# A gated attention and expert block on one core: transposes moved from the DMA engines to TensorE, and the experts' down products regrouped

## The chip, the cores and the metric

The kernel runs on one core of a Trainium2 chip. The metric is the device time of one execution in microseconds; three timed runs of the kernel before gave 570.42, 572.45 and 572.47, the median is 572.45. The profile is of one further execution. Engines are named as in the profile: PE is TensorE, PEld its weight loads, DVE is VectorE, ACT is ScalarE, POOL is GpSimd, SP is SyncE, which here only issues DMAs.

## The reference, cut to what matters

Inputs are tokens `x` of 4 batches x 512 x 512 (H = 512), a wide weight per batch (`fside`, 512 x 512), a narrow weight per batch (`ctx`, 512 x 256), a router weight for 16 experts, three weights for each expert (I = 352), and a shared pair of layers (704 wide).

```python
def _smooth_quant_linear(x, w):          # per batch, int8 steps
    s = sqrt(max(amax_x, EPS) / max(amax_w, EPS)); xs = x / s; ws = w * s
    x_scale, w_scale = row maxima / 127
    x_q, w_q = round(xs / x_scale), round(ws / w_scale)
    return x_q @ w_q.T * x_scale * w_scale.T
...
x = x + tanh(g_xattn) * linear2(silu(gate) * up)        # gate, up = halves of linear1(layernorm(x))
t = layernorm(x)
top 2 of softmax(t @ gate_w.T); tokens sorted to 16 experts x 256 slots
expert_out = (silu(buf @ w_gate) * (buf @ w_up)) @ w_down
x = x + tanh(g_ffn) * (weighted sum of a token's two expert rows + shared layers(t))
```

## The kernel before, in words

**Stages.** The work falls into five stretches of the profile's time.

1. The opening, up to about 62 us, is batch 0's quantized layers, written out by hand as a list of steps with a rough time each (`opening.at`), and ends with `beside` (line 1316), which puts batch 1's first steps among the first chunk of batch 0's shared layers.
2. From 62 to 282 us a planner (`Plan`, before the kernel function) sets the order. Each step has an engine, a cost in us, the steps it needs, the buffers that it takes and gives, and a rank; the planner plays the engines forward and takes, among the steps that are ready, the one with the lowest rank. What it yields is only the order in which each engine's instructions stand; the engines then follow it strictly, each waiting for what its next instruction needs. Here run batches 1 to 3 of the quantized layers (`plan_first`, `plan_second`), the routing (`plan_scores`), and, with the highest rank numbers, the shared layers of batches 0 to 2 (`plan_shared`), which fill TensorE.
3. From 282 to 511 us the 16 experts follow each other in a loop (`gate_up`, `down_routed`, `turn_features`).
4. From 511 to the end come the shared layers of batch 3 and the gathering of the experts' rows into the result.

**Quantized layers.** `steps_x` (line 509) and `steps_w` (556) write int16 steps. A product needs them with the summed dimension in partitions, so they are turned. For batches 0 and 1, TensorE turns them as bf16 bit patterns into a PSUM bank, four or two 128x128 blocks for each of four tiles (`turn_tile`, line 356), and ScalarE or VectorE copies the bank to SBUF as numbers (`take_x`, `take_w`, `take_a`). For batches 2 and 3 (`BY_DMA`, line 363), SP issues DMA transposes of two tiles each (`send_pair`, 369), which land on the X-bar path, and VectorE casts the landed int16 to bf16 in place (`steps_to_float`, 380). `block` picks the matching layout for the product.

**Normalized tokens.** After the second layer, `normal` (746) writes a tile `y`. `keep_normal` (759) splits each f32 of `y` into two planes of 16 bits with a ScalarE copy, and `store_normal` (764) writes the planes to `xn_dram`. `plan_keep` (1429) plans both, for most tiles with a late rank. `turn_normal` (770) turns `y` on TensorE for the router and the shared layers.

**Experts.** For expert e, `gather(e, h)` (1102), issued on GpSimd's queue, fetches 128 rows of planes by index into `xg`; `send_tokens` (1129) issues a DMA transpose on SP's queue into `xp`; `join_tokens` (1133), a strided ScalarE copy, puts the planes together to `A`, the turned f32 tokens. Tokens of e + 1 are prepared while e is computed. `combine_tokens` (1136) and `combine_weights` (1086) make the sums and differences, on VectorE, with which gate and up need seven products in place of eight (a scheme of Winograd's kind); in `gate_up` (1183) they are written to four banks b1 to b4, and ScalarE and VectorE copies and adds gather them. b1 is accumulated on while copies are taken of it: each later product onto b1 stands behind a ScalarE copy. Then `down_tile` (1234) makes two tiles of 128 tokens x 512 from three chunks of the 352 features (128, 128 and 96 rows), `take_down` (1163) copies them out of PSUM and ScalarE's queue issues their store, and `turn_features` (1168) turns the gated features of e with six TensorE turns, which `join_features` (1177) copies to SBUF with VectorE. In the loop, expert e's gate and up stand first, then down of e - 1, then the turns of e:

```python
        for e in range(E - 1):
            gate_up(e)
            if e > 0:
                down_routed(e - 1)
            turn_features(e)
...
        gate_up(E - 1)
        down_tile(E - 2, 0)
        turn_features(E - 1)
        down_tile(E - 2, 1)
```

Weight loads from DRAM are issued on SP's queue two experts ahead (`load_gate`, `load_up`, `load_down`, from line 1071).

Of the kernel before, what the change touches and what calls it, by code (L numbers as in the profile page):

```python
# [12 lines left out]
I16 = mybir.dt.int16  # L13
# [107 lines left out]
def flamingo_gated_kernel(  # L121
# [32 lines left out]

    xn_dram = dram.tile([B * S, 2 * H], I16, tag="xn_dram", name="xn_dram")
# [207 lines left out]
    BY_DMA = (2, 3)  # L363

    def by_tile(dst):

        return dst.rearrange("p k s -> p (k s)").rearrange("p (t k q) -> p t k q", t=TT, q=P)

    def send_pair(dst, q, u):

        to = by_tile(dst.bitcast(I16))[:, 2 * u : 2 * u + 2].rearrange("p t k q -> p (t k) q")
        nc.sync.dma_start_transpose(out=to, in_=q[:, 2 * u : 2 * u + 2, :].rearrange("p t n -> p (t n)"))

    def block(b, dst, k, t=None):

        if b not in BY_DMA:
            return dst[:, k, :] if t is None else dst[:, k, bass.ts(t, P)]
        return by_tile(dst)[:, :, k, :] if t is None else by_tile(dst)[:, t, k, :]

    def steps_to_float(dst):  # L380

        vec.tensor_copy(dst, dst.bitcast(I16))

    def planes(on, dst, src):

        n = src.shape[1]
        copy_on(on, dst[:, :, :n], src.bitcast(I16).rearrange("p (n l) -> p l n", l=2))

    def turn_planes(dst, src):

        nc.sync.dma_start_transpose(out=dst, in_=src.rearrange("p l n -> p (l n)"))

    def join_planes(on, dst, src):

        copy_on(on, dst.bitcast(I16).rearrange("p k (s l) -> p l k s", l=2), src.rearrange("p (l k) s -> p l k s", l=2))

# [43 lines left out]
    def first(b):  # L440
# [93 lines left out]
        def send_x(u):  # L534
            send_pair(w.xqT, v.xq, u)

        def send_w(u):
            send_pair(w.wqT, v.wq, u)

        def sent_x():  # L540
            steps_to_float(w.xqT)

        def sent_w():
            steps_to_float(w.wqT)

# [24 lines left out]
        def product(t):  # L570
            if t == 0:
                w.a3 = qb.tile([P, TT, A], F32, tag="a3", name="a3")
                w.ama = qb.tile([P, A], F32, tag="ama", name="ama")
            accs[t] = chain_ps[1]([P, H], F32, "acc")
            for k in range(HC):
                pe.matmul(  # L576
                    accs[t], lhsT=block(b, w.xqT, k, t), rhs=block(b, w.wqT, k), start=(k == 0), stop=(k == HC - 1)
                )
# [37 lines left out]
    def second(b):  # L616
# [66 lines left out]
        def send_a(u):  # L683
            send_pair(v.xqT, v.xq, u)

        def send_w(u):
            send_pair(v.wqT, v.wq, u)

        def sent_a():
            steps_to_float(v.xqT)  # L690

        def sent_w():
            steps_to_float(v.wqT)

# [26 lines left out]
        def multiplied(t):  # L721
            if t == 0:
                v.mv = stat.tile([P, TT, 2], F32, tag="mv2", name="mv2")
            accs[t] = chain_ps[1]([P, H], F32, "acc2")
            for k in range(nk):
                pe.matmul(  # L726
                    accs[t], lhsT=block(b, v.xqT, k, t), rhs=block(b, v.wqT, k), start=(k == 0), stop=(k == nk - 1)
                )
# [28 lines left out]
        yps = {}  # L757

        def keep_normal(t, on=act):
            yp = qb.tile([P, 2, H], I16, tag="q", name="yp", bufs=2)  # L760
            planes(on, yp, ys[t])
            yps[t] = yp.rearrange("p l n -> p (l n)")

        def store_normal(t):
            j = b * TT + t
            nc.sync.dma_start(out=xn_dram[j * P : (j + 1) * P, :], in_=yps[t])
# [335 lines left out]
    def gather(e, h):  # L1102
        c = e * (CAP // P) + h
        R[e].xg[h] = xg = ep.tile([P, 2, H], I16, tag="xg", name="xg", bufs=3)
        pool.indirect_dma_start(  # L1105
            out=xg.rearrange("p l n -> p (l n)"),
# [8 lines left out]
    def open_routed():  # L1115
        home.A = shp.tile([P, 2, CAP // P, HC, P], F32, tag="xT", name="xgT", bufs=2)
        home.S4 = qb.tile([P, 4, HALF, P], F32, tag="a3", name="S4")
        home.xp = [ep.tile([P, 2 * HC, P], I16, tag="xp", name="xp", bufs=2) for _ in range(CAP // P)]
# [10 lines left out]
    def send_tokens(e, h):  # L1129
        R[e].A = home.A[:, e % 2]  # L1130
        turn_planes(home.xp[h], R[e].xg[h])

    def join_tokens(e, h, on=act):
        join_planes(on, R[e].A[:, h], home.xp[h])
# [42 lines left out]
    def join_features(e, h):  # L1177
        r = R[e]
        if h == 0:
            r.hT = qb.tile([P, len(CHUNKS_I), CAP], F32, tag="wc", name="ehT", bufs=2)  # L1180
        vec.tensor_copy(r.hT[:, :, bass.ts(h, P)], r.tps[h][:, : len(CHUNKS_I), :])

    def gate_up(e):
# [7 lines left out]
        if e > 1:  # L1191
            take_down(e - 2, 1)
        for h in range(CAP // P):
            if two_more:
                gather(e + 2, h)
            if more:
                send_tokens(e + 1, h)
        product(b1, r.A11, r.Bg, True)
        act.copy(p1, b1)
        product(b2, r.A12, r.Dg, True)  # L1200
        if two_more:
# [8 lines left out]
        if e > 0:  # L1210
            for h in range(CAP // P):
                join_features(e - 1, h)
# [4 lines left out]
        product(b4, r.S4, r.Du, True)  # L1217
        if two_more:
# [3 lines left out]
        if more:  # L1222
            for h in range(CAP // P):
                join_tokens(e + 1, h)
        product(b1, r.A22, r.T4, False)
        act.activation(g2, b1, AF.Silu)
        for step in weights[2:]:
            step()
        vec.tensor_tensor(home.h[1][:, :I], g2, u3, ALU.mult)
        if more:  # L1230
            for step in combine_tokens(e + 1):
                step()

# [6 lines left out]

    def down_routed(e):
        for h in range(CAP // P):
            down_tile(e, h)
        take_down(e, 0)
        if e + 2 < E:
            load_down(e + 2)
# [63 lines left out]
    for t in range(TT):  # L1310
        opening.at(61.0 + 0.5 * t, lambda t=t: s0.normal(t, vec), lambda t=t: s0.turn_y(t))
# [4 lines left out]
    def beside():  # L1316
# [3 lines left out]
        order += up[:2] + [f1.row_rs, f1.row_s, *each(f1.multiply), *each(f1.divide)] + up[2:] + [times]  # L1320
# [4 lines left out]
    opening.at(65.0, beside, lambda: s0.keep_normal(TT - 1), lambda: s0.store_normal(TT - 1))  # L1325
# [10 lines left out]
    SENT = 1.8  # L1336

    def plan_sent(send, sent, us, steps, q, rank, needs=()):

        landed = []  # L1340
        for u in range(TT // 2):
            issue = plan.add("SP", 1.3, lambda u=u: send(u), *steps[2 * u : 2 * u + 2], *needs, rank=rank)
            landed.append(plan.add("XBAR", 0.8, nothing, issue, rank=rank, gives=[q]))
        done = plan.add("DVE", us, sent, *landed, rank=rank)
        done.late = SENT
        return [done]
# [14 lines left out]
    def plan_first(b, f, wide, narrow, began):  # L1361

        add, r = plan.add, b * 1000.0
        by_dma = b in BY_DMA
# [30 lines left out]
        if by_dma:  # L1395
            turns, took = [], plan_sent(f.send_x, f.sent_x, 0.7, steps, q, r + 10, [first_last[b - 1]])
        else:
            o = add("PE", 0.0, f.open_x, steps[0], rank=r + 10, takes="tp", count=2)
            turns = [add("PE", 0.27, lambda t=t: f.turn_x_tile(t), steps[t], o, rank=r + 10, gives=[q]) for t in range(TT)]
            took = [add("ACT", 1.02, lambda: f.take_x(0, act), *turns, rank=r + 11, gives=[o]), add("DVE", 0.7, lambda: f.take_x(2, vec), *turns, rank=r + 11, gives=[o])]  # L1400
# [5 lines left out]
        if by_dma:  # L1406
            took += plan_sent(f.send_w, f.sent_w, 0.7, steps, q, r + 13, [first_last[b - 1]])
        else:
            o = add("PE", 0.0, f.open_w, steps[0], *turns, rank=r + 13, takes="tp", count=2)
            turns = [add("PE", 0.27, lambda t=t: f.turn_w_tile(t), steps[t], o, rank=r + 13, gives=[q]) for t in range(TT)]  # L1410
            took += [add("ACT", 1.02, lambda: f.take_w(0, act), *turns, rank=r + 14, gives=[o]), add("DVE", 0.7, lambda: f.take_w(2, vec), *turns, rank=r + 14, gives=[o])]
# [17 lines left out]
    def plan_keep(s, t, y, rank):  # L1429

        kept = plan.add("ACT", 1.1, lambda t=t: s.keep_normal(t), y, rank=rank, takes="q2", gives=[y])
        sent = plan.add("SP", 0.45, lambda t=t: s.store_normal(t), kept, rank=rank)
        STORED.append(plan.add("XBAR", 0.0, nothing, sent, rank=rank, gives=[kept]))
        STORED[-1].late = 2.3

    def plan_second(b, s, first):
# [14 lines left out]
        by_dma = b in BY_DMA  # L1451
        steps = [add("ACT", 0.5, step, n, rank=r + 1) for step in each(s.steps_a)]
        A_free[b + 1] = steps[-1]
        if by_dma:
            took = plan_sent(s.send_a, s.sent_a, 0.43, steps, q, r + 1)
        else:
            o = add("PE", 0.0, s.open_a, steps[0], rank=r + 1, takes="tp")
            turns = [add("PE", 0.22, lambda t=t: s.turn_a_tile(t), steps[t], o, rank=r + 1, gives=[q]) for t in range(TT)]
            took = [add("ACT", 1.02, lambda: s.take_a(act), *turns, rank=r + 1, gives=[o])]
# [4 lines left out]
        if by_dma:  # L1464
            took += plan_sent(s.send_w, s.sent_w, 0.43, steps, q, r + 2)
        else:
            o = add("PE", 0.0, s.open_w, steps[0], rank=r + 2, takes="tp")
            turns = [add("PE", 0.22, lambda t=t: s.turn_w_tile(t), steps[t], o, rank=r + 2, gives=[q]) for t in range(HC)]
# [398 lines left out]
```

## Time and profile before

| What | Value |
|---|---|
| median of three runs | 572.45 us (570.42 to 572.47) |
| the profiled execution | 570.75 us, of which the span (first to last instruction) is 568.7 |
| granted TensorE clock, mean | 0.987 |
| DMA transposes | 32 of routed tokens, 16 of steps |
| ScalarE copies `xgT<-xp` | 31, 1.34 us each |
| ScalarE copies `yp<-y` | 16, 1.05 us each |
| VectorE casts after a DMA transpose of steps | 8, 0.41 to 1.33 us each |
| POOL waiting for `xp<-xg` before a gather | 161.0 us in 16 waits |

The profile's parts give busy time by engine (1), the span in 40 slices (2), DMA queues (3), the chain of work that ended last, followed back from the last instruction (4), and instruction groups with the idle time before them (5). Queries of the trace give the same for a stretch, an instruction list in order of time, and the chain piece by piece. Matmuls are pipelined: the mean length of one in a group is longer than the distance between two, so prices are taken from pieces of the chain.

### The profile page before, as it was taken

Reading aid. Unit: us, or ns where it says so; the run is one execution under the profiler, and the core shown is the slowest. Engines: PE = TensorE matmul, PEld = TensorE weight load, DVE = VectorE, ACT = ScalarE, POOL = GpSimd, SP = SyncE. Lnnn points to the kernel's source line nnn. Section 1 sums busy time; section 2 is a strip of 40 time slices with the busy share of each in tenths; the row PEclk is TensorE's granted clock in tenths of the full one; section 3 lists DMA queues with packets and bytes.
Section 4 is the critical chain, followed back from the end, with each engine's and each line's share of the span. In section 5 each row is a group of like instructions: output and inputs, shape, how many; then the busy total and the mean of one; then the engine's idle time right before and its main releaser. Section 6 shows DMA issues by size and latency. Waiting matters only on the chain.

```text
span 568.7 us, 6298 instructions
## 1 busy us (share of the span) xinstructions
PE 536.9 (94%) x1946; PEld 297.6 (52%) x1946; DVE 423.4 (74%) x976; ACT 234.1 (41%) x399; POOL 140.2 (25%) x155
## 2 busy tenths in 40 slices
PE   3786799999999999999989999999999999999997
PEld 2653444544445454454455555555555555557852
DVE  6999788999998998986278666666666666535887
ACT  4464567537626173060136444444444444422310
POOL 1315032253151511200320111111111110006771
PEclk8699999999999999999999999999999999999999
DMA  8981012012304184010676999999999989315778
GB/s 275 373 260 37 1 74 75 0 39 75 73 1 76 37 281 131 5 74 1 142 208 226 265 266 259 269 257 262 283 265 265 262 255 250 101 55 166 197 234 311
DMA packets 93969, 95.09 MB, mean 167 GB/s; under 512 B 51552, under 2 KB 70240, under 8 KB 93936
## 3 DMA queue, kind: packets, MB, share of 16 engines
q1 hardware_dynamic: 84064, 69.39, 44.6%
q0 software_dynamic: 5120, 16.78, 9.4%
q10 hardware_dynamic: 4752, 8.52, 4.0%
q8 instruction: 16, 0.26, 0.2%
q14 instruction: 17, 0.14, 0.1%
HBM read 66.36 MB, written 16.78 MB: 146 GB/s over the span
## 4 chain that ended last, share of the span: by engine, by line
PE 84%; DVE 12%; issue 1%; ACT 1%; DMA 1%; POOL 0%; SPq 0%; DVEq 0%
PE b L1154 23%; PE eo L987 15%; PE sh L1037 11%; PE pg L972 9%; PE pu L972 9%; PE b L1732 4%; PE pr L1011 2%; PE tp_h L1174 2%; PE acc L576 2%; PE sh L1043 1%; PE rowb L307 1%; DVE scx L331 1%; DVE xn L494 1%; PE tp_am L299 1%; PE acc L726 1%
## 5 line engine op out<-in xcount | busy, mean ns | idle before, releaser
L987 PE MATMUL eo<-wd,ehT 128*128 128x512 f32 (+1 forms) x192 | 85.1, 592 | 0.0
L1105 POOL DMA_INDIRECT xg<-xn_dram,slot_token x32 | 34.6, 1082 | 195.8 <-DMA xp<-xg 161.0
L1037 PE MATMUL sh<-wsd,hT 128*128 128x512 f32 x160 | 73.9, 597 | 0.0
L987 PEld LDWEIGHTS eo<-wd,ehT 128*128 128x128 f32 (+1 forms) x192 | 36.4, 190 | 41.6 <-issue 36.5
L972 PE MATMUL pg<-xT,wsg 128*128 128x512 f32 x120 | 57.4, 599 | 0.7 <-ACT xT L354 0.7
L972 PE MATMUL pu<-xT,wsu 128*128 128x512 f32 x120 | 56.5, 596 | 0.0
L1203 DVE TENSOR_TENSOR p<-p,b 128x352 f32<-128x352 f32 x16 | 8.3, 520 | 59.4 <-PE b L1154 59.4
L354 ACT COPY xgT<-xp 128x1024 int16<-128x1024 int16 x31 | 39.5, 1339 | 24.5 <-DMA xp<-xg 24.4
L1784 POOL DMA_INDIRECT yk<-eo_dram,slot x32 | 33.2, 1038 | 52.2 <-PE b L1732 42.8
L1037 PEld LDWEIGHTS sh<-wsd,hT 128*128 128x128 f32 x160 | 28.9, 190 | 30.9 <-issue 28.7
L1154 PE MATMUL b<-T,S 128*128 128x352 f32 x128 | 40.6, 460 | 0.7 <-DVE S L1145 0.7
L1154 PE MATMUL b<-wg,xgT 128*128 128x352 f32 x128 | 40.6, 460 | 0.0
L1154 PE MATMUL b<-wu,S 128*128 128x352 f32 x128 | 40.5, 459 | 0.0
L1165 ACT COPY eo_sb<-eo 128x512 f32<-128x512 f32 x32 | 18.7, 585 | 50.4 <-PE eo L987 40.5
L972 PEld LDWEIGHTS pu<-xT,wsu 128*128 128x128 f32 x120 | 21.6, 190 | 21.2 <-issue 21.0
L972 PEld LDWEIGHTS pg<-xT,wsg 128*128 128x128 f32 x120 | 21.1, 190 | 21.4 <-issue 19.9
L1154 PEld LDWEIGHTS b<-T,S 128*128 128x128 f32 x128 | 24.2, 190 | 14.5 <-issue 1.2
L1154 PEld LDWEIGHTS b<-wu,S 128*128 128x128 f32 x128 | 24.3, 190 | 13.5
L499 POOL TENSOR_TENSOR wi<-wi,s_row 128x512 f32<-128x512 f32 x16 | 19.9, 1276 | 42.7 <-ACT s_row L484 42.7
L1154 PEld LDWEIGHTS b<-wg,xgT 128*128 128x128 f32 x128 | 23.1, 190 | 10.9 <-issue 0.8
L739 POOL TENSOR_TENSOR X<-X,o 128x512 f32<-128x512 f32 x13 | 17.1, 1342 | 35.7 <-DVE o L732 35.7
L292 DVE BATCH_NORM_STATS2 bn<-X 128x6 f32<-128x512 f32 x32 | 21.7, 677 | 4.7 <-DMA X<-in_x_dram 4.3
(262 smaller groups left out, 957.5 us busy)
## 6 DMA issues: line engine op xcount, KB each, us to landing
wg<-in_L_ffn_w_gate_dram SPq DMA_DIRECT2D x16, 704.0 KB, 5.0
wu<-in_L_ffn_w_up_dram SPq DMA_DIRECT2D x16, 704.0 KB, 6.2
wd<-in_L_ffn_w_down_dram SPq DMA_DIRECT2D x16, 512.0 KB, 4.6
eo_dram<-eo_sb ACTq DMA_DIRECT2D x32, 256.0 KB, 3.9
X<-in_x_dram SPq DMA_DIRECT2D x16, 256.0 KB, 5.3
xn_dram<-yp SPq DMA_DIRECT2D x16, 256.0 KB, 2.0
out_dram<-X SPq DMA_DIRECT2D x15, 256.0 KB, 5.4
wi<-in_fside_BxS2xS_dram SPq DMA_DIRECT2D x3, 1024.0 KB, 6.4
```

The source lines that it names most:

```text
L292: vec.bn_stats(st, src)
L354: return (vec.tensor_copy if on is vec else act.copy)(dst, src)
L499: on.tensor_tensor(w.wi[:, t, :], w.wi[:, t, :], v.s_row, ALU.mult)
L739: on.tensor_tensor(Xb[:, t, :], Xb[:, t, :], os_[t], ALU.add)
L972: pe.matmul(v.ps[name], lhsT=w[:, k, o : o + P], rhs=xT[:, k, :], start=(k == 0), stop=(k == HC - 1))
L987: pe.matmul(acc, lhsT=hT[:m, c, bass.ts(t, P)], rhs=wd[:m, c, :], start=(c == 0), stop=(c == len(chunks) - 1))
L1037: pe.matmul(accs[t], lhsT=s.hT[:, c, bass.ts(t, P)], rhs=wsd[:, c, :], start=(c == 0), stop=(c == last))
L1105: pool.indirect_dma_start(out=xg.rearrange("p l n -> p (l n)"), out_offset=None, in_=xn_dram, in_offset=bass.IndirectOffsetOnAxis(ap=slot_ ...
L1154: pe.matmul(ps[:, :I], lhsT=lhs[:, k, :], rhs=rhs[:, k, :], start=(first and k == 0), stop=(k == HALF - 1), skip_group_check=not first,)
L1165: act.copy(eo, R[e].acc[h])
L1732: pe.matmul(ps, lhsT=w[:, k, :], rhs=x[:, k, :], start=(first and k == 0), stop=(k == HALF - 1), skip_group_check=not first,)
L1784: pool.indirect_dma_start(out=yk, out_offset=None, in_=eo_dram, in_offset=bass.IndirectOffsetOnAxis(ap=slot[i % 2][:, tiles[i // 2] : tile ...
```

## The change

Four things are changed.

- Batches 2 and 3 go the way of batches 0 and 1: all DMA transposes of steps, their casts, and the layout helper `block` are removed, and the planner plans TensorE turns and copies for all batches.
- `keep_normal` is removed; `xn_dram` holds f32 rows and `store_normal` writes `y` itself, which batch 0 does in the opening and the later batches in the plan, without the late rank. `gather` fetches f32 rows (four `xg` buffers in place of three). `turn_tokens` turns a gathered tile with four f32 turns into a PSUM bank and `take_tokens` copies it out.
- For e - 1 = 0 to 13 the down product is made inside `gate_up(e)`: the first 256 features as seven products of 128 tokens x 256 columns, with sums of features from VectorE (`combine_features`) and differences of weights from GpSimd (`combine_down_weights`); the last 96 features as four ordinary products of 256 columns. `join_features` moves from VectorE to ScalarE there. The last two weight differences of the next expert move between the new products.
- In two places TensorE's order changes: in `beside`, all `up` passes of the chunk now stand ahead of the two row broadcasts; and `turn_features(e - 1)` now stands in `gate_up(e)`, behind the first two products.

The diff, cut to its core (left out: removed helpers and the removed `by_dma` branches of the planner):

```diff
-    xn_dram = dram.tile([B * S, 2 * H], I16, tag="xn_dram", name="xn_dram")
+    xn_dram = dram.tile([B * S, H], F32, tag="xn_dram", name="xn_dram")
...
-            nc.sync.dma_start(out=xn_dram[j * P : (j + 1) * P, :], in_=yps[t])
+            nc.sync.dma_start(out=xn_dram[j * P : (j + 1) * P, :], in_=ys[t])
...
-        R[e].xg[h] = xg = ep.tile([P, 2, H], I16, tag="xg", name="xg", bufs=3)
+        R[e].xg[h] = xg = ep.tile([P, H], F32, tag="xg", name="xg", bufs=4)
...
+    def turn_tokens(e, h):
+        r = R[e]
+        if h == 0:
+            r.A, r.xtp = home.A[:, e % 2], {}
+        r.xtp[h] = tp = ps_t.tile([P, HC, P], F32, tag="tp", name="tp_xg")
+        for k in range(HC):
+            pe.transpose(tp[:, k, :], r.xg[h][:, bass.ts(k, P)], ident)
+
+    def take_tokens(e, h, on=act):
+        copy_on(on, R[e].A[:, h], R[e].xtp[h])
...
     def gate_up(e):
...
-        if e > 1:
-            take_down(e - 2, 1)
+
+        d = e - 1 if 0 < e < E - 1 else None
         for h in range(CAP // P):
             if two_more:
                 gather(e + 2, h)
-            if more:
-                send_tokens(e + 1, h)
+        if d is not None:
+            combine_down_weights(d)
         product(b1, r.A11, r.Bg, True)
         act.copy(p1, b1)
         product(b2, r.A12, r.Dg, True)
+        if e > 0:
+            turn_features(e - 1)
...
-                join_features(e - 1, h)
+                join_features(e - 1, h, act.copy)
...
         product(b4, r.S4, r.Du, True)
+        if more:
+            for h in range(CAP // P):
+                turn_tokens(e + 1, h)
+                take_tokens(e + 1, h)
...
         vec.tensor_tensor(home.h[0][:, :I], g1, u2, ALU.mult)
-        if more:
-            for h in range(CAP // P):
-                join_tokens(e + 1, h)
...
+        else:
+            combine_features(d)
+            product(b1, r.A22, r.T4, False)
+            act.activation(g2, b1, AF.Silu)
+            vec.tensor_tensor(home.h[1][:, :I], g2, u3, ALU.mult)
+            down_of_halves(d, (b3, b4), weights[2:])
...
+    def combine_features(e):
...
+            (r.dS[0], r.F21, r.F22, ALU.add),
+            (r.dS[1], r.dS[0], r.F11, ALU.subtract),
+            (r.dS[2], r.F11, r.F21, ALU.subtract),
+            (r.dS[3], r.F12, r.dS[1], ALU.subtract),
...
+            vec.tensor_tensor(out, one, other, op)
...
+    def combine_down_weights(e):
...
+            (r.dT[0], r.W12, r.W11),
+            (r.dT[1], r.W22, r.dT[0]),
+            (r.dT[2], r.W22, r.W12),
+            (r.dT[3], r.W21, r.dT[1]),
...
+            pool.tensor_tensor(out, one, other, ALU.subtract)
...
+    def down_of_halves(e, banks, weights):
...
+        product(b1, r.F11, r.W11)
+        act.copy(p1, b1)
+        product(b2, r.F12, r.W21, last=False)
+        rest(b2, 0, 0, first=False)
+        vec.tensor_tensor(eo[0][:, : H // 2], p1, b2, ALU.add)
+        product(b1, S2, T2, first=False, more=True)
+        act.copy(u2, b1)
+        weights[0]()
+        product(b3, S1, T1)
+        vec.tensor_tensor(u2, u2, b3, ALU.add)
+        rest(b4, 0, 1, last=False)
+        product(b1, S3, T3, first=False, more=True)
+        act.copy(u3, b1)
+        product(b4, S4, r.W22, first=False)
+        vec.tensor_tensor(eo[0][:, H // 2 :], u2, b4, ALU.add)
+        rest(b3, 1, 1, first=False, more=True)
+        vec.tensor_tensor(eo[1][:, H // 2 :], u3, b3, ALU.add)
+        rest(b1, 1, 0, first=False, last=False, more=True)
+        product(b1, r.F22, T4, first=False, more=True)
+        weights[1]()
+        act.copy(eo[1][:, : H // 2], b1)
+        for h in range(2):
+            nc.scalar.dma_start(out=eo_dram[e * CAP + h * P : e * CAP + (h + 1) * P, :], in_=eo[h])
+        if e + 2 < E:
+            load_down(e + 2)
...
-        order += up[:2] + [f1.row_rs, f1.row_s, *each(f1.multiply), *each(f1.divide)] + up[2:] + [times]
+        order += up + [f1.row_rs, f1.row_s, *each(f1.multiply), *each(f1.divide), times]
...
         for e in range(E - 1):
             gate_up(e)
-            if e > 0:
-                down_routed(e - 1)
-            turn_features(e)
```

## The prediction

> **What bounds the kernel now.** I read the profile from the outside in: busy share by engine, then the chain of work that ended last, then busy time by stage, then that chain and TensorE's timeline inside the stages that the change touches. Page, part 1 and part 4:
>
> ```profile
> PE 536.9 (94%) x1946; PEld 297.6 (52%) x1946; DVE 423.4 (74%) x976; ACT 234.1 (41%) x399; POOL 140.2 (25%) x155
> ...
> PE 84%; DVE 12%; issue 1%; ACT 1%; DMA 1%; POOL 0%; SPq 0%; DVEq 0%
> ```
>
> TensorE (PE) is 84% of the chain and no DMA wait is in it to speak of, though the busy DMA slices on the page invite that guess. Busy time by stage (columns: stretch, its length, then PE, weight loads, VectorE, ScalarE, GpSimd busy, the granted clock, DMA share, GB/s):
>
> ```profile
> 62.00:85.00 23.00, 20.64 (x83) 10.08 (x84) 17.49 (x38) 15.05 (x26) 4.98 (x4) 1.00 0.12 46
> 85.00:282.00 197.00, 196.34 (x687) 92.46 (x685) 165.66 (x461) 84.84 (x147) 55.08 (x59) 1.00 0.26 70
> 282.00:296.00 14.00, 11.84 (x44) 7.24 (x43) 11.26 (x21) 5.04 (x8) 2.09 (x3) 1.00 0.90 245
> 296.00:494.00 198.00, 198.00 (x648) 115.26 (x647) 124.90 (x236) 84.47 (x129) 27.60 (x25) 1.00 0.90 247
> ```
>
> From 85 to 494 us TensorE is idle for about 3 us in all, at full clock. The DMA transposes load the DMA engines (0.90 in the expert stage) but nobody on the chain waits for them. One expert in the chain (start, length, what, instructions):
>
> ```profile
> 406.15 0.66 PE tp_h L1174 x6
> 406.80 8.29 PE b L1154 x28
> 415.09 5.16 PE eo L987 x12
> 420.24 0.66 PE tp_h L1174 x6
> ```
>
> The three pieces are the whole period: 8.29 + 5.16 + 0.66 = 14.1 us. An f32 product is two passes in the records (14 calls, 28 instructions), so a pass of 352 columns takes 0.296 and one of 512 takes 0.43 us. Whatever is added to TensorE here is added to the end.
>
> **Prices.** Three come from pieces of the same chain:
>
> ```profile
> 510.65 6.04 PE b L1732 x28
> ...
> 243.57 0.87 PE tp_x L773 x8
> ...
> 83.32 0.45 PE tp_q L361 x8
> ```
>
> A pass of 256 columns: 6.04/28 = 0.216. An f32 turn of a 128x128 block: 0.87/8 = 0.109 (the feature turns give the same, 0.66/6). A bf16 turn: 0.45/8 = 0.056; the next piece then shows 0.91 instead of 0.86 for two passes, so a group costs some 0.05 more.
>
> [...] The row is: six feature turns in 0.66 us, clock 1.00, although the group's mean is 273 ns each, because they are pipelined. [...] The row's spacing decides for me.
>
> **Part by part, on TensorE.**
>
> 1. Routed tokens turned on TensorE: 16 experts x 2 tiles x 4 blocks = 128 turns x 0.109 = **+13.9**. They replace 32 DMA transposes, which the chain does not contain, so nothing comes back there. Of the 128, 120 lie in the expert stage, where TensorE has no idle time; the first eight lie before it, among products without gaps.
>
> 2. Batches 2 and 3: 16 + 16 + 8 + 8 = 48 bf16 turns each, 96 in all. Lower end 96 x 0.056 = 5.4. Upper end by batch 1, which already goes this way: groups of four at 0.22 + 0.05 for x and the wide weight (8 x 0.27 = 2.2), 0.55 for a, 0.89 for the narrow weight, whose turns waited for VectorE: 3.6 a batch, 7.2. I take **+6.5**.
>
> 3. Seven products for 14 experts: 6 calls of 512 columns (12 x 0.43 = 5.16) become 7 + 4 calls of 256 (22 x 0.216 = 4.75): -0.41 x 14 = **-5.7**. The four "rest" calls have 96 rows; the 96-row calls of the old loop lie inside the 5.16 at the same 0.43, so rows do not change the price. Weight loads go from 12 to 22 at 0.19 each, 4.2 us beside 4.75 us of passes; the 28 passes above show such loads hidden behind 256 columns.
>
> 4. The two filled waits, and one that falls away. TensorE's timeline, wait and releaser in brackets:
>
> ```profile
> 70.65 0.65 PE L307 MATMUL rowb<-ident,rs 128*128 128x128 f32 x4 [1.94 <-DVE rs L325]
> ...
> 285.28 2.60 PE L1154 MATMUL b<-T,S 128*128 128x352 f32 x8 [0.67 <-DVE S L1145]
> ...
> 293.46 0.55 PE L1174 MATMUL tp_h<-ident,h_e 128*128 128x128 f32 x3 [1.49 <-DVE h_e L1229]
> ```
>
> At 70.65 the other four `up` passes (1.72 us) move ahead of the broadcast that waits 1.94: **-1.7**. At 293.46 the turns of expert 0 waited for the gated features; they now stand behind two products (2.37 us) of expert 1: **-1.5**. At 285.28 the sums of expert 0's tokens came late, after gathers, two DMA transposes and their copies from 271.3 on. Gather, turn (0.44) and copy (0.58) are shorter than that, so I count this wait as gone: **-0.7**.
>
> Sum: 13.9 + 6.5 - 5.7 - 1.7 - 1.5 - 0.7 = **+10.8**. In the steady stage a period goes from 14.1 to 8.29 + 0.66 + 0.87 + 4.75 = **14.57**.
>
> **What must stay hidden beside it.** In one period of 14.57:
> - VectorE: 124.9/198 x 14.1 = 8.9 us now; minus two feature copies (2 x 0.51), plus four sums of 128x128 (0.28 each, by the 128-column one-hot row) and four adds of 256 columns (0.42): 10.7. It fits.
> - ScalarE: minus two joins (1.34) and two 512-column copies (0.585); plus two token copies (0.58), two feature copies of 384 columns (between 0.45 for 352 and 0.585 for 512; 0.48), four copies of 256 (0.37): about level. The eo stores stay on its queue and wait for VectorE's and its own last halves; the next thing behind them is the copy p1, needed 3.0 us into the next period. Cover is over a microsecond.
> - GpSimd: gathers no longer wait for DMA transposes (161 us of waiting now, all idle time), then four 128x256 differences at 0.72: 2.9 us, needed about 11 us later. The next gathers stand behind them and have a period of slack.
> - SP: loses 32 transposes of about 1.5 us each and the loads follow each other; the down weights still have a full period. In the front, 16 copies (1.05) leave ScalarE, and stores go straight from `y`; a `y` buffer is then held for its store, 2.0 us. Neither engine bounds that stage.
>
> The new waits that I can't read off are inside the seven products. One 256-column bank is accumulated on while copies are taken from it. After S2·T2 the third product has 0.86 us of other passes ahead of it, against one copy of 0.37 plus about 0.2 of latency: covered. The tightest is the rest product into b3: it is queued behind VectorE's add u2 += b3, which is queued behind the first half of eo (0.42) and a weight difference (0.89). Counting from the end of F12·W21 and its rest: 0.16 drain + 0.42 + 0.89 + 0.42 and three gaps of 0.04 give 2.0 us; TensorE arrives after five products of two passes, 5 x 0.43 = 2.15. Cover 0.1 to 0.2. Bounds for an expert: nothing, or up to one GpSimd operation of 0.72 if it holds VectorE up:
>
> ```profile
> 231.33 1.27 POOL L739 TENSOR_TENSOR X<-X,o 128x512 f32<-128x512 f32 x1 [10.47 <-DVE o L732]
> ...
> 231.95 1.20 DVE L739 TENSOR_TENSOR X<-X,o 128x512 f32<-128x512 f32 x1
> ```
>
> A VectorE sum of two 512-column SBUF tiles takes 0.69 alone (0.68 and 0.69 at lines 1711 and 1712); beside GpSimd it took 1.20, ending 0.55 after GpSimd did. [...] The GpSimd differences wait for the matmuls that read the previous ones, so their first can start just as the weight difference runs, mostly behind it. I take 0.07 us an expert, **+1.0**, nearest to nothing.
>
> Forecast: +11.8. On the profiled execution, span 568.7 and 570.75 with what lies around it, that is 580.5 and 582.6. The median of the runs, 572.45, is 1.7 above that execution and the lowest run 0.3 below it, so the median after may lie from 582 to 584: I say **583.0**. Own range, from the ends of parts 2 to 4 and the wait: 579 to 588.
>
> **Rivals.**
> - B, a wait in the products replaces the ones removed: GpSimd pushes VectorE back and the rest product waits 0.5 to 0.72 for each of 14 experts, +7 to +10: about 591. For it: the cover of 0.15. Against: VectorE reaches that difference first.
> - C, the front is late: the order there comes from the planner, and turns that reach TensorE ahead of their steps hold up everything behind them. Batch 1 waited 1.2 us in all for x steps; four such sets at 1 to 2 us give +6: about 589.
> - D, the seven products do not shorten anything: if weight loads of 0.19 are not hidden where a bank must be freed, four a call chain, -0.41 becomes 0 or worse: +5.7, about 589. Against: the 28 passes at 0.216.
> - E, not slower: the turns come almost free, their streaming hidden beside weight loads and drains. The turns are 20.4 of the bill and all else sums to -8.6, so it decides at a turn price of 42% of mine (0.046 for an f32 block); with free turns about 563. Against: 0.66 us for six turns stands in every period between two pieces that have no gap. Filled waits alone can't do it: all TensorE idle time after 62 us, 9.7 us in four stretches, is less than the turns.
>
> **Chances.** Forecast 0.69, B 0.13, C 0.07, D 0.05, E 0.06. The range reaches from the low end of the forecast less a little of E to the upper end of B: 577 to 592. Half a per cent (2.9 us) is about what a measurement here can tell from no change; of E I give 0.04 to faster and 0.02 to the same, the rest is slower: 0.94.
>
> **What will show it.** The expert period in the chain: 14.57 if right, near 15.2 under B or D. Under B, a wait of TensorE or its loads on VectorE's u2 in the new products; under D, no wait but more than 0.216 a pass. The token turns eight in 0.87 us (far less under E). The first expert's products should begin 4 to 5 us later than the 282 us of now; later still is C. Wrong altogether I would be if some stage had a TensorE bound that the DMA transposes were slowing; but a 512-column pass takes 0.43 at a DMA share of 0.26 as at 0.90.

## The result and the profile after

The changed kernel takes **595.88 us** in the median (594.15 to 597.29, 4 runs), the kernel before 571.92 (570.42 to 572.47, 4 runs): ratio 1.0422 (1.0384 to 1.0460), 24.0 us slower. Forecast were 11.8, and the range ended at 592. The direction was right, the size was half of it. The profiled execution after has a span of 594.9 beside 568.7, +26.2; it lies 0.75 above its median, that of before 1.2 below.

Page of the kernel after, parts 1 and 4:

```profile
PE 556.5 (94%) x2310; PEld 345.2 (58%) x2310; DVE 456.5 (77%) x1056; ACT 219.8 (37%) x447; POOL 188.8 (32%) x211
...
PE 75%; DVE 16%; DMA 2%; ACT 2%; issue 2%; SPq 1%; POOL 0%; ACTq 0%; DVEq 0%
```

TensorE has only 19.6 us more of busy time than before, and its share of the chain fell from 84 to 75%: part of the new time is waiting. Busy time by stage, the same columns as in the prediction, shows where:

```profile
62.00:85.00 23.00, 21.68 (x88) 10.74 (x89) 18.30 (x40) 11.91 (x23) 4.98 (x4) 1.00 0.04 15
85.00:282.00 197.00, 187.75 (x739) 91.63 (x737) 162.14 (x455) 76.76 (x139) 54.02 (x58) 0.98 0.16 52
282.00:296.00 14.00, 14.00 (x41) 6.21 (x41) 3.62 (x7) 0.58 (x1) 1.89 (x2) 1.00 0.14 39
296.00:494.00 198.00, 195.46 (x842) 142.91 (x841) 149.29 (x293) 75.72 (x172) 73.89 (x78) 1.00 0.64 208
```

From 85 to 282 us TensorE is idle for 9.2 us (0.7 before), and the clock is 0.98 there. At 296 to 494 it is idle for 2.5 (none before). The steady expert period, on the other hand, is what was forecast. The chain around two of them (start, length, what):

```profile
428.87 2.37 PE b L1094 x8
...
431.89 4.74 PE b L1094 x16
436.62 0.87 PE tp_xg L1071 x8
437.50 1.19 PE b L1094 x4
438.68 1.73 PE db L1226 x8
...
443.44 2.37 PE b L1094 x8
```

443.44 - 428.87 = 14.57, the forecast's own figure. Eight token turns take 0.87 and eight passes of the new down product 1.73, that is 0.216 each.

For a table of where the time came in, I read the first product of each expert off TensorE's timeline:

| | first expert begins | period of expert 0 | of expert 1 | of expert 2 | of the others | last expert begins |
|---|---|---|---|---|---|---|
| before | 281.98 | 11.87 | 14.10 | 14.10 | 14.10 | 491.23 |
| after | 299.26 | 9.27 | 15.94 | 16.78 | 14.58 | 516.31 |
| after minus before | **+17.3** | -2.6 | +1.8 | +2.7 | +0.48 | +25.1 |

The first expert begins 17.3 us later; forecast were 4 to 5 in the prediction's last section, while its own terms make 5.7 (6.5 + 0.87 - 1.7).

**The front.** After's timelines, first TensorE, then ScalarE, then the DMA issues on SP's queue:

```profile
214.18 1.12 PE L729 MATMUL tp_l<-ident,parts 128*128 128x128 f32 x4 [7.50 <-ACT parts L724]
```

```profile
213.54 0.59 ACT L724 COPY parts<-logit 128x512 f32<-128x512 f32 x1 [11.16 <-DMA xn_dram<-y]
```

```profile
196.69 0.38 SPq L1008 DMA_DIRECT2D wg<-in_L_ffn_w_gate_dram  x1
...
202.34 0.70 SPq L1017 DMA_DIRECT2D wd<-in_L_ffn_w_down_dram  x1
203.15 3.38 SPq L700 DMA_DIRECT2D xn_dram<-y  x3
```

`parts`, a copy of the router's scores, takes a buffer of the ring of three that `y` uses too. A `y` is now free only when its store has read it. Three stores of batch 2 stand on SP's queue behind the loads of the first two experts (4.2 MB), and the chain has `203.15 10.31 DMA xn_dram<-y`: 10.3 us to landing where the page's median is 2.6. In the kernel before, the ScalarE copy `yp` stood in between and released `y`; there it was `yp` that waited (6.94 us), with nothing on the chain behind it. ScalarE's timeline before:

```profile
208.22 0.58 ACT L790 COPY parts<-logit 128x512 f32<-128x512 f32 x1
...
216.69 1.05 ACT L354 COPY yp<-y 128x1024 int16<-128x1024 int16 x1 [6.94 <-DMA xn_dram<-yp]
```

So the sign stood in the profile before: there, too, three stores stand behind the same loads on SP's queue, and the slowest landed 8.5 us after its issue, against a median of 2.0.

After the 7.50 us wait the clock is down: the granted clock is 0.50 from 212 to 216 us and 0.51 from 216 to 218, four f32 turns take 1.12 instead of 0.44, and six passes of `sh` 3.96 instead of 2.58. In `b1_steps_pe`, below, it is 0.50 behind a wait of 2.49 us.

**Experts 1 and 2.** TensorE's waits there:

```profile
312.24 2.60 PE L1094 MATMUL b<-T,S 128*128 128x352 f32 x8 [0.53 <-DVE S L1085]
315.18 2.63 PE L1094 MATMUL b<-wu,S 128*128 128x352 f32 x8 [0.33 <-ACT u L1148]
...
328.01 2.63 PE L1094 MATMUL b<-T,S 128*128 128x352 f32 x8 [0.36 <-ACT p L1139]
331.96 2.63 PE L1094 MATMUL b<-wu,S 128*128 128x352 f32 x8 [1.32 <-ACT u L1148]
```

In expert 1 the token sums on VectorE run beside GpSimd's first weight differences (VectorE's timeline, then GpSimd's):

```profile
309.73 1.50 DVE L1084 TENSOR_TENSOR S<-xgT 128x256 f32<-128x256 f32 x1
```

```profile
310.20 0.73 POOL L1211 TENSOR_TENSOR dT<-wd 128x256 f32<-128x256 f32 x1
```

The sums take 1.50, 0.84, 0.94 and 0.94 us beside GpSimd's four differences of 0.73 to 0.91, and the first of them began 0.47 us ahead of GpSimd's first. With no GpSimd instruction beside them they take 0.42 (three sums of expert 2, from 326.23 us on). In expert 2, `routing_weights` puts an Exp between two table loads into ScalarE's queue:

```profile
325.90 1.28 ACT L886 ACT_TABLE_LOAD   x1 [0.86 <-DVE T L1033]
...
327.97 1.28 ACT L1147 ACT_TABLE_LOAD   x1
```

It stood there before, too, but behind 5.16 us of down product that TensorE could do meanwhile. Now the down product is inside `gate_up`, ahead of it, and the first copies of the next expert come late.

### The profile page after: what moved, and what is told of

It is laid out like the page before. It is cut to its first block, busy times and chain, and to the rows that moved or that the text cites. A ratio compares the mean times of both kernels' runs of the same rounds, so it can differ in the third digit from the quotient of the medians.

```text
span 594.9 us, 7204 instructions
## 1 busy us (share of the span) xinstructions
PE 556.5 (94%) x2310; PEld 345.2 (58%) x2310; DVE 456.5 (77%) x1056; ACT 219.8 (37%) x447; POOL 188.8 (32%) x211
## 3 DMA queue, kind: packets, MB, share of 16 engines
q0 software_dynamic: 5120, 16.78, 9.0%
HBM read 66.36 MB, written 16.78 MB: 140 GB/s over the span
## 4 chain that ended last, share of the span: by engine, by line
PE 75%; DVE 16%; DMA 2%; ACT 2%; issue 2%; SPq 1%; POOL 0%; ACTq 0%; DVEq 0%
PE b L1094 21%; PE sh L971 10%; PE db L1226 7%; PE pg L906 7%; PE pu L906 6%; PE b L1226 4%; PE b L1714 4%; PE tp_xg L1071 2%; PE pr L945 2%; PE eo L921 2%; DMA xn_dram<-y 2%; PE tp_h L1114 2%; PE sh L977 1%; DVE scx L330 1%; DVE xn L459 1%
## 5 line engine op out<-in xcount | busy, mean ns | idle before, releaser
L906 PE MATMUL pu<-xT,wsu 128*128 128x512 f32 x120 | 57.7, 599 | 0.0
L1211 POOL TENSOR_TENSOR dT<-wd 128x256 f32<-128x256 f32 x28 | 23.8, 852 | 24.0 <-PE b L1226 24.0
L1226 PE MATMUL db<-wd,ehT 128*128 128x256 f32 (+1 forms) x112 | 28.7, 379 | 0.0
L1211 POOL TENSOR_TENSOR dT<-wd,dT 128x256 f32<-128x256 f32 x28 | 25.9, 923 | 3.7 <-PE db L1226 2.6
L353 ACT COPY xgT<-tp_xg 128x512 f32<-128x512 f32 x31 | 16.7, 588 | 23.4 <-PE tp_xg L1071 23.4
L1226 PEld LDWEIGHTS db<-wd,ehT 128*128 128x128 f32 (+1 forms) x112 | 21.3, 190 | 5.2
```

The lines of the kernel that those rows point to most:

```text
L353: return (vec.tensor_copy if on is vec else act.copy)(dst, src)
L906: pe.matmul(v.ps[name], lhsT=w[:, k, o : o + P], rhs=xT[:, k, :], start=(k == 0), stop=(k == HC - 1))
L1211: pool.tensor_tensor(out, one, other, ALU.subtract)
L1226: pe.matmul(ps, lhsT=lhs, rhs=rhs, start=first, stop=last, skip_group_check=more)
```

## The experiments

Two theories, to be told apart. **S and C** (stores and cover): the prices are right; the excess is the stores behind the loads, and the covers lost in experts 1 and 2. **P** (prices): the turns in front cost far more than forecast, or the seven products save nothing. `a1` to `a4` and `b1` to `b3` ran on chips on which the kernel before takes 592.3 us, `a0`, `a6` and `b4` on one where it takes 571.5; every ratio is against the kernel before on the same chip (the reason is in the last section).

**1. The place of the stores.** `a1_loads_late`: the changed kernel, the loads of the first experts planned behind batch 2's stores.

```diff
-    weights_there = plan.add("SP", 3.0, experts_weights, firsts[B - 1].last)
+    weights_there = plan.add("SP", 3.0, experts_weights, firsts[B - 1].last, *STORED[4:8])
```

> The changed kernel with one edit: the planner issues the experts' first weight loads behind the four stores of y of batch 2, so SP issues the same instructions in another order and no other engine's order changes. Theory (SP order): in the changed kernel the copy parts waits 11.2 us for a y buffer, because three stores stand on SP behind eight loads and land 10.3 us late; TensorE waits 7.5 us for it and then runs slowly for a while. With the stores ahead both go: 9 to 10 us less than the changed kernel, 585 to 587. Rival (front late by the new TensorE turns, rival C of the prediction): the turns cost the time and the copy was late anyway: less than 3 us less, 593 or more.

`a2_store_actq`: batch 2's stores are issued on ScalarE's queue instead.

```diff
-            nc.sync.dma_start(out=xn_dram[j * P : (j + 1) * P, :], in_=ys[t])
+            (nc.scalar if b == 2 else nc.sync).dma_start(out=xn_dram[j * P : (j + 1) * P, :], in_=ys[t])
```

> The changed kernel with one edit: the four stores of y of batch 2 are issued on ScalarE's queue in place of SP's; the expert loads stay where they are. If only the place on SP's queue delays the stores, they land 2 to 4 us after their issue and this is as fast as with late loads, 585 to 587. If the loads' transfers, 4 MB in flight on the DMA engines, delay them too, a store lands 6 us or more after its issue and a part of the 7.5 us wait stays: 588 to 593.

Ratios 1.0271 (1.0235 to 1.0307) and 1.0270 (1.0235 to 1.0306): both take back some 8.5 us of the 24, a little less than the 9 to 10 expected of the first. The first expert begins at 291.12 and 290.29. Busy time by stage from 185 to 236 us, after and then with the loads late:

```profile
185.00:236.00 51.00, 42.72 (x178) 20.59 (x177) 38.53 (x123) 14.85 (x28) 13.00 (x15) 0.93 0.32 106
```

```profile
185.00:236.00 51.00, 50.22 (x202) 23.94 (x201) 46.48 (x142) 16.46 (x31) 16.73 (x17) 1.00 0.31 106
```

TensorE's idle time and the slow clock (0.93) go together, with the same 106 GB/s moved. But the place on SP's queue is not the whole delay: in `a2` batch 2's stores, beside the loads on another queue, landed 2.4 to 7.2 us after their issue, 6.5 in the median, as the second expectation had it, where with late loads they landed after 2.2 to 3.9. They were issued from 196.6 us on and not from 203.15, so that `parts` waited only 2.3 us and TensorE not at all for it. Waiting behind the loads and running beside them together made TensorE wait; taking away the first was enough.

**2. Experts 1 and 2.** `a3_routing_end`: the routing weights stand behind the last expert's gate and up.

```diff
-            if e == 1:
-                routing_weights(qb)
...
         gate_up(E - 1)
+        routing_weights(qb)
+        table(AF.Silu)
```

> The changed kernel with one edit: the routing weights (one Exp on ScalarE with two table loads, and VectorE sums) are computed after the last expert's gate and up in place of after expert 1's. Theory: in the changed kernel their old cover, the down product behind them, is gone, and TensorE waits 0.36 and 1.32 us in expert 2 by the trace: 1.5 to 2.5 us less, 593.5 to 594.5. Rival: the table loads cost the same wherever they stand: no difference over 0.5 us.

`a4_three`: this, the loads late, and the weight differences of expert 0 made ahead of the loop.

```diff
-        if d is not None:
+        if d is not None and d > 0:
             combine_down_weights(d)
...
         open_features()
+        combine_down_weights(0)
```

> The changed kernel with three edits: late expert loads, routing weights at the end, and expert 0's down weight differences computed by GpSimd before the expert loop in place of in expert 1, where they slowed VectorE's token sums from 0.42 to 0.84 to 1.50 us and TensorE waited 0.5 and 0.3. If these three waits are all that the prediction missed, 9.5 + 2 + 1.2 us less than the changed kernel: 582 to 584, which is where the prediction's sum of TensorE work stands. If the sum itself was too low, 587 or more.

Ratios 1.0397 (1.0367 to 1.0428) and 1.0213 (1.0177 to 1.0249). Routing late brings expert 2 to 14.57 and leaves expert 1 at 15.95; its total gains only about 1.5 us (0.25%) on after's ratio, less than the interval, so for it the periods decide and not the time. In a4 all periods from expert 1 on are 14.57 or 14.58, the first expert begins at 289.76, and +12.1 us are left, beside the forecast's +11.8. That they are so near is in part luck: the front is still 2.1 later than forecast, and 1.0 was forecast for waits in the seven products that did not come.

**3. Parts of the change in the kernel before.** `b1_steps_pe`: `BY_DMA = ()`, steps of batches 2 and 3 turned on TensorE.

> The kernel before with one edit: batches 2 and 3 turn their steps on TensorE (BY_DMA empty), all else as before. The prediction's price for this part is +6.5 us (5.4 to 7.2), so 577 to 579.5. If the planner's new order makes TensorE wait at batch edges (rival C), 582 or more. If the turns are nearly free (rival E), 573 or less.

Ratio 1.018 (1.0159 to 1.0200), +10.7 instead of +6.5. The first expert begins at 295.37. ScalarE's timeline, then TensorE's:

```profile
225.75 1.04 ACT L354 COPY yp<-y 128x1024 int16<-128x1024 int16 x1 [13.26 <-DMA xn_dram<-yp]
```

```profile
227.53 1.08 PE L361 MATMUL tp_q<-ident_h,aq 128*128 128x128 bf16 x6 [2.49 <-ACT aq L351]
```

The same stores, behind the same loads, here hold the copy `yp`, and behind it on ScalarE's queue the steps that the new turns need: 2.7 us of waits, and behind them a granted clock of 0.50 from 230 to 232 us. In this execution the clock was also 0.50 from 72 to 74 us, behind a wait of 1.94 that the kernel before has at full clock. The first expert begins 13.4 later than before: 0.4 from the opening, 2.7 of waits and 10.3 of TensorE's busy time. In the 10.3 the turns and the slow clock are not parted; with the forecast's 6.5 for the turns, 3.8 would be the clock. So this run does not settle the price of the turns; `a6_old_down` does, below, whose front had no slow clock. The medians differ by less than 13.4, as expert 0 gives back 0.9 (10.97 beside 11.87) and the profiled execution lies 0.8 above its median; some 1.0 stays open.

`b2_waits`: the two waits filled by order, as in the change.

> The kernel before with the two changes of TensorE's order alone: all up passes ahead of the row broadcasts, and the feature turns of an expert behind the next expert's first two products. The prediction's price: -1.7 and -1.5, so 568.5 to 569.5. By the changed kernel's trace the first gives back 0.68 at the router product, which now waits for the copy s_row: then -2.5, 569.5. If the waits only move: within 1 us of before.

Ratio 0.9959 (0.9945 to 0.9973), -2.4 us by it and -3.0 by the medians, as expected (-2.5). The first expert begins at 281.85, as before, but the opening was 0.4 longer here. Counted from the first product of the shared layers, at 62.86 and 62.42 us, the first expert begins after 218.99 instead of 219.56, and the shared layers behind the experts after 445.69 instead of 448.07 (they begin at 508.55 and 510.49). So the first wait brought 0.6 of its 1.7, and the experts 1.8. Counted so, like fronts agree: 218.91 and 218.89 in `b3` and `b4`, which have the same order; 227.30 and 227.27 in `a1` and `a4`, whose first experts begin 1.4 apart.

**4. The changed kernel again, and with the old down product.** `a0_changed` is the changed kernel, unaltered.

> The changed kernel itself, unaltered, on the chip of the other runs, so that they are compared with it and not only through the kernel before. Expected: some 24 us over the kernel before of the same chip (ratio 1.040 to 1.042), first expert product near 299, steady period 14.58, periods of experts 1 and 2 near 15.9 and 16.8.

Ratio 1.0432 (1.0398 to 1.0465); the first expert at 297.58, the wait for `parts` 6.4, periods 15.95, 16.44 and 14.58: reproduced.

`a6_old_down`: loads late, and the down product outside `gate_up`, as it was.

```diff
-        d = e - 1 if 0 < e < E - 1 else None
+        d = None
+        if e > 1:
+            take_down(e - 2, 1)
...
             gate_up(e)
+            if e > 0:
+                down_routed(e - 1)
             if e == 1:
                 routing_weights(qb)
```

> The changed kernel with the experts' loads behind batch 2's stores, and the down projection of all experts in its old form (two tiles, 6 calls of 512 columns an expert); the routing weights stay where they are. Theory (seven products save 0.41 us an expert, but take the cover from the routing weights in expert 2 and bring GpSimd beside VectorE's token sums in expert 1): steady period 14.58 + 0.41 = 14.98; expert 2 falls from 16.45 to the period, for 5.16 us of down product stand behind its gate and up again; expert 1 loses its 1.36 too. Against the kernel with the loads late alone: 14 x 0.41 = +5.7, minus 1.9, minus 1.4, so +2.4, some 18.1 over the kernel before (ratio 1.031). Rival (the loss in expert 2 is the price of the activation tables themselves, and not of the missing cover): expert 2 stays about 1.9 over the period, +4.3 instead of +2.4, ratio 1.034. Rival (seven products save nothing): period stays 14.58 and the time falls below the kernel with the loads late.

Ratio 1.0288 (1.0256 to 1.0321), +17.0 where the theory had +18.1; the rival's ratio of 1.034 lies outside the interval. The chain, with the starts of experts 2, 3 and 4 right behind the down product `eo`:

```profile
309.01 5.16 PE eo L921 x12
314.16 2.37 PE b L1094 x8
...
323.98 5.16 PE eo L921 x12
329.14 2.37 PE b L1094 x8
...
338.95 5.16 PE eo L921 x12
344.11 2.37 PE b L1094 x8
```

329.14 - 314.16 = 14.98, and 14.97 for the next: expert 2 has no loss at all, although the routing weights and their two table loads are where they were, and expert 1 has none either. So the loss is the missing cover. And 14.98 - 14.57 = 0.41: the seven products save what was forecast.

**5. Seven products with the DMA transposes kept.** `b3_seven`: the kernel before, with the two orders of b2, the seven products, the routing weights at the end, expert 0's differences ahead of the loop, and the second copy of the turned tokens (`join_tokens`) between the products.

> The kernel before, DMA transposes kept, with the two changes of order, the seven products for 14 experts, the routing weights at the end, and expert 0's weight differences ahead of the loop; the second join of an expert stands between the new products. TensorE's sum: 14 x -0.41 = -5.7 and -2.5 for the order: 563 to 565, faster than both kernels, period 8.29 + 0.66 + 4.75 = 13.70. Rival: ScalarE, with joins of 1.34 us beside the new copies, holds the bank copies up: a period of 14.1 or more, 569 or more.

Ratio 0.9987 (0.9963 to 1.0011): 0.8 us less, which is no difference that can be told, and a miss. Undisturbed periods are 13.70, 0.40 below before, but the others reach 17.71. ScalarE's timeline and then TensorE's in that one:

```profile
342.70 1.33 ACT L354 COPY xgT<-xp 128x1024 int16<-128x1024 int16 x1 [3.25 <-DMA xp<-xg]
343.90 0.45 ACT L1240 ACTIVATE g<-b 128x352 f32<-128x352 f32 x1
344.25 0.36 ACT L1296 COPY dp<-db 128x256 f32<-128x256 f32 x1
```

```profile
344.71 0.67 PE L1289 MATMUL db<-dT,dS 128*128 128x256 f32 x2 [2.09 <-issue]
```

The token copy waits for a DMA transpose, and the bank copy `dp`, which the third product needs, stands behind it. The profile calls TensorE's wait "issue"; it ends where `dp` does. `b4_send_early`: each transpose is sent right after the copy that frees its buffer, ahead of the next down weights on SP's queue.

```diff
-            if more:
-                send_tokens(e + 1, h)
+            if e == 0:
+                send_tokens(1, h)
...
+        def join(h):
+            join_tokens(e + 1, h)
+            if two_more:
+                send_tokens(e + 2, h)
```

> The kernel before with its DMA transposes, the two waits filled, seven products (as the earlier run of that kind), and each DMA transpose of an expert's tokens sent right behind the join that frees its buffer, ahead of the next down weights on SP's queue, some 3 to 5 us earlier. In the earlier run undisturbed periods took 13.70 and disturbed ones 14 to 17.7, where ScalarE waited for a transpose and stood ahead of the joins that TensorE's banks need. Theory (the transposes were only sent too late): all periods 13.70, that is 14 x 0.40 = 5.6 less than the kernel with the two waits filled; with those 3.0 some 583.7 beside 592.3 (ratio 0.985). Rival (the DMA engines, 0.90 busy in the expert stage, carry no shorter period): periods still near 14.1 to 14.3, time 589 to 592, ratio 0.995 to 1.000, and the saving of the seven products can only be had with the tokens turned elsewhere.

Ratio **0.9856** (0.9830 to 0.9883): 563.47 us beside 571.5, as expected, and the best of all the kernels here. Chain and busy time by stage:

```profile
441.04 2.37 PE b L1156 x8
...
454.74 2.37 PE b L1156 x8
```

```profile
356.00:490.00 134.00, 134.00 (x549) 98.56 (x548) 105.90 (x213) 68.08 (x127) 47.06 (x52) 1.00 0.98 252
```

The period is 13.70 for experts 2 to 13. The DMA engines are 0.98 busy, and TensorE waits for none of it: when the transposes were sent had been the limit, not the DMA engines. From 290 to 500 us ScalarE waits 15.6 us for transposes in `b3` and not at all in `b4`. The two ran on different chips, and neither was run on the other's; but `before` and `b2`, one on each kind, have the same period of 14.10, and their transposes landed after 6.1 and 6.2 us.

## Why the prediction failed, and what in it was right

In spans, 26.2 were measured and 11.8 forecast. By stage:

| | forecast | measured | difference |
|---|---|---|---|
| up to the first expert | 7.4 turns - 1.7 wait = 5.7 | 17.3 | 11.6 |
| from there to the end | 13.05 turns - 5.7 - 1.5 - 0.7 + 1.0 = 6.1 | 8.9 | 2.8 |

The medians differ by 24.0 and not by 26.2: the profiled executions, one above and one below its median, account for some 2 of these 14.4.

- **Right: the prices.** The period is 14.57 as worked out; a turn costs 0.109 and a pass of 256 columns 0.216. In front, TensorE's busy time from 60 us to the first expert is 225.9 with the old down product and 218.5 in before: +7.4, as forecast (6.5 and 0.87), at a granted clock of 1.00 in both. So rivals D and E are out, and so is theory P.
- **Right: no wait inside the seven products.** No wait of TensorE in them is in the trace after: its waits from 280 to 520 us, 2.5 in all, are those in gate and up of experts 1 and 2. No run of the changed kernel shows the +1.0 forecast for it (0.07 an expert), nor rival B.
- **The step that failed** is this one: "stores go straight from `y`; a `y` buffer is then held for its store, 2.0 us. Neither engine bounds that stage." It took the page's median landing for a store that stands behind 4.2 MB of loads on SP's queue, and asked for engines where a buffer was the bound. Measured: a landing of 10.3 us, a wait of TensorE of 7.5, and a slow clock for 2 more. Between after and the kernel with the old down product (the same front but for the loads) the first expert moves by 9.5 us: 7.4 of TensorE's idle time and 2.1 of slower work.
- **The wait at 70.65, -1.7:** from 60 to 90 us TensorE's idle time fell only from 2.83 to 1.80, for the next instruction now waits 0.68 for ScalarE's `s_row`. Together with small new gaps after 156 us (1.4, of which 0.6 for `ama`) the front loses 2.1 more. That closes the 11.6.
- **A second step that failed: what must stay hidden** was worked out for the steady period only. The one expert that has the routing weights in it lost its cover, +2.2 (1.9 in `a0`, `a1` and `a2`), and the one in which GpSimd's differences start with nothing ahead of them runs beside the token sums, +1.4. The latter is what rival B names, GpSimd holding VectorE up, but in the token sums of one expert and not in the products of 14. With 0.15 in one late expert, and without the 1.0 that never came, they make 2.7 of the 2.8.
- **Rival C** (the front is late through the planner's order): the front is late, by 11.6 where C had some 6, but not by turns that reach TensorE ahead of their steps. What the planner had priced wrongly was a store, at 0.45 us to issue and 2.3 to land.

## What to carry to other kernels

When a copy between a buffer and its store is removed, the buffer is held for as long as the store waits on its queue: follow that queue past everything that was put on it earlier, and do not take the median landing. When work moves from behind a step into its front, look at every step that it used to cover, the ones that come only once above all. And a transfer off the chain that ends just in time is worth sending earlier, before its work is moved to the engine that is the bound: sent some 6 us earlier, the DMA transposes let the seven products bring a ratio of 0.9856 in place of 0.9987, where the turns on TensorE cost 13.9 us.

## What had not been expected of the hardware

- **Chips.** On the chips of `a1` to `a4` and `b1` to `b3` the kernel before takes 592.3 us, on the others 571.5. The 20 us are one place in the tail, while GpSimd issues the gathers of the results one after the other: in b2_waits TensorE, ScalarE and VectorE start little between about 521 and 545 us. The chain of b2_waits, which names what it cannot place "another core or an unknown queue":

```profile
521.26 5.25 another core or an unknown queue
...
526.91 13.59 another core or an unknown queue
...
540.91 3.81 another core or an unknown queue
```

  They go on between 540 and 545 us; the gathers pause from 541 on. No event in the trace releases them, and I did not try what does, so the cause is open; the front and the expert stage are the same on both kinds of chip (first expert 281.98 and 281.85).
- **DMA engines at 0.98** over 134 us, two DMA transposes an expert among them, cost TensorE nothing, once the transposes were sent in time: in `b4_send_early` it was busy for all of the 134.00 us.
